# Two gathered blocks per expert in one tile, the shared expert ahead of routing, convolution biases added to x, fixed-point weights in the gated layer's columns

## The chip, the cores and the metric

The kernel runs on one core of a Trainium2 chip. The metric is the device time in microseconds (us) of one launch. The engines are named as in the profile: PE (TensorE; PEld are its weight loads), DVE (VectorE), ACT (ScalarE), POOL (GpSimd, which issues the indirect gathers) and SP (SyncE, which issues most other DMAs). An engine works through its instructions in a fixed order.

## The reference

A decoder of four layers on x of 8 batches x 256 tokens x 256 features. Each layer is attention, attention to a context, and a feed-forward part; after each the layer norm of x plus the result is taken:

```python
x = _layernorm(x + _L1_ffn_ref(x, gate_w, w_gate_up, w_down, shared_w_gate_up, shared_w_down))
...
x = _layernorm(x + _L2_ffn_ref(x, Wq, keys, down_embed, up_embed, Wg, Wu, Wd))
x = _layernorm(x + _L3_attn_ref(x, in_proj_w, in_proj_b, conv_w, ..., out_proj_w, out_proj_b, ln_w, ln_b))
x = _layernorm(x + _L3_xattn_ref(x, ctx_768, Wq, Wk, Wv, Wo, bo))
x = _layernorm(x + _L3_ffn_ref(x, w1, b1, w2, b2))
```

The parts that the change touches are these.

- `_L1_ffn_ref`: 32 experts with 4 chosen per token and room for 256 tokens each. An expert is silu(x Wg) * (x Wu), then Wd. A shared expert of the same form works on every token.
- `_L2_ffn_ref`: a gated feed-forward part (Wg, Wu, Wd with 1024 hidden columns), plus 4 heads x 8 single-row experts per token, taken from a table of 4096 rows.
- `_L3_attn_ref`: a projection to u and v, a short convolution and a linear recurrence over time, a projection out with a bias, then h = out + x, and (h - mean) * rsqrt(var + eps) * ln_w + ln_b. The outer line adds x once more and norms again.
- `_L3_ffn_ref`: 256 to 1024 to 256 with values rounded to multiples of 2^-8 and a piecewise linear gelu.

## The kernel before, in words

x stands in SBUF twice: `X` (tokens on partitions, 16 tiles of 128 x 256) and its transpose `xT`. `finish` (L183 and on) takes a sum z, norms it into `X`, turns it on PE and copies it to `xT` on ACT. The program is written in a framework that tracks the tiles and, at build, puts the instructions of each engine in order: by their place in the program, filling gaps with later ones that its own simulated timeline holds to be ready. So work of different layers stands interleaved on the engines, and the order doesn't change at run time. A pool's memory passes to a later pool when the tiles of the earlier one are released. Float32 matmuls show as two records each in the profile, transposes as one.

**Layer 1's feed-forward** (`l1_ffn`). `route1` makes one-hot matrices of the chosen experts on DVE, counts places with small matmuls (L1163, L1164), and finds with 16 x 4 matmuls (L1190, fed by `at` from DVE and ACT) which token goes to which place: `take` (L1197). Then the shared expert's hidden values `shT` are computed for eight chunks of 256 tokens: 8 matmuls of 128x128 by 128x256 to `ph` (L139, through `mm`; 64 records in all are `ph<-xT,sgu`), a silu on ACT (L1126) and a product on DVE (L1127). Then the loop over the 32 experts: SP loads the expert's weights `we` (L1266); `gathered_T` (L991 and on) is called twice, once per block of 128 tokens, and each call gathers 128 rows (L983, POOL), turns them with two transposes (L998) and copies them to `xeT` (L1000, ACT); 8 matmuls with 128 moving columns make `ph` (128x128 x512 records over all experts), silu and product make `hT`, two matmuls make `py`, DVE copies it to `y` (L1283), and SP stores it. After each fourth expert two tiles of the shared expert are projected down and added to `X` (L1291). The work pool has three buffers of each name, so three `xe` tiles are one and a half experts. DVE also works off the preparation of layer 2's quantized weights (L1877 to L1939) in the gaps.

**Layer 2's experts and layer 3's attention** (`l2_ffn`). For each of the 8 batches `expert_batches` runs the gated part (L1523 and on), then 64 gathers of table rows (L983, `rows`), dot products on DVE (L1511), `diag` on ACT (L1562) and matmuls into `po` (L1563). The convolution (`convolution_batches`) and the context attention (`context_batches`) of the batch before are Python generators, and a piece of them is issued between pieces of the experts (`next(later, None)`). In the convolution's last part the projection out has a bias matmul with one row (L141, through `mm`), then z = po + x (L1625), norm statistics, and five DVE instructions: two at L1628, and L1631, L1632 and L1633.

**Layer 3's feed-forward** (`fixed_point`). Its weights `w4` are loaded by SP after the loop over the batches, into the weight tile of which layer 2's weights are the last user (L125, L129). The pools `f3`, `f3w` and `f3p` come after those of the experts. Its matmuls are `ph<-xT,w`, its first activation is L1761, and it goes through 16 units, two for each batch.

Of the kernel before, what the change touches and what calls it, by code (L numbers as in the profile page):

```python
# [11 lines left out]
F32 = mybir.dt.float32  # L12
# [4 lines left out]
ALU = mybir.AluOpType  # L17
AX = mybir.AxisListType
PSUM = bass.MemoryType.PSUM
# [23 lines left out]
class Net:  # L43
# [947 lines left out]
    def gathered_T(self, xd, index, work):  # L991

        nc = self.nc
        xe = work.tile([P, D], F32, name="xe")
        self.gather_rows(xe, xd, index)
        pt = self.ps_t.tile([P, 2, P], F32, name="pt")
        for c in range(2):
            nc.tensor.transpose(pt[:, c, :], xe[:, c * P : (c + 1) * P], self.ident)  # L998
        xeT = work.tile([P, 2, P], F32, name="xeT")
        nc.scalar.copy(xeT, pt)  # L1000
        return xeT


# [226 lines left out]
    def l1_ffn(self, w):  # L1230
        nc, tc = self.nc, self.tc
        E, K, C = 32, 4, 256
        DROP = E * C
        with (
            tc.tile_pool(name="f1", bufs=1) as keep,
            tc.tile_pool(name="f1w", bufs=3) as work,
            ExitStack() as ctx,
        ):
            sgu = keep.tile([P, 2, 256], F32, name="sgu")
            nc.sync.dma_start(sgu, self.ins["l1f_sgu"].rearrange("p (c n) -> p c n", c=2))  # L1240
            sd = keep.tile([P, D], F32, name="sd")
            nc.sync.dma_start(sd, self.ins["l1f_sd"])
            xd, yd = self.xd1, self.yd1
            nc.gpsimd.partition_all_reduce(self.w_scale, self.w_sums[:, : len(L2X)], P, bass_isa.ReduceOp.add)
            with (
                tc.tile_pool(name="f1q", bufs=1) as pool,
                tc.tile_pool(name="f1r", bufs=1, space=PSUM) as ps,
            ):
                take = self.route1(E, K, C, pool, work, ps, keep)
            pool = ctx.enter_context(tc.tile_pool(name="f1l", bufs=1))  # L1250
            none = pool.tile([1, D], F32, name="none")
            nc.vector.memset(none, 0.0)
            nc.scalar.dma_start(yd[DROP : DROP + 1, :], none)
            with tc.tile_pool(name="f1p", bufs=2, space=PSUM) as ps:
                shT = pool.tile([P, NTOK], F32, name="shT")
                for o in range(0, NTOK, 256):
                    ph = ps.tile([P, 2, 256], F32, name="ph")
                    for m in range(2):
                        self.mm(
                            ph[:, m, :],  # L1260
                            [(sgu[:, c, m * P : (m + 1) * P], self.xT[:, c, o : o + 256]) for c in range(2)],
                        )
# [183 lines left out]
    def l2_ffn(self, w):  # L1446


        tc = self.tc
        with ExitStack() as ctx:  # L1450
            w3 = self.load(
                ("l3a_win", 2), ("l3a_wout", 2), ("l3x_wq", 2), ("l3x_wo", 4),
                rows=("l3a_bout", "l3a_ln_w", "l3a_ln_b", "l3x_bo"), spare=8 * D,
            )
            win, wout, wq, wo, bout, ln_w, ln_b, bo, fifth = w3
            pool3 = ctx.enter_context(tc.tile_pool(name="a3", bufs=1))
            ps3 = ctx.enter_context(tc.tile_pool(name="a3p", bufs=2, space=PSUM))
            convolve = self.convolution_batches((win, wout, bout, ln_w, ln_b), pool3, ps3)
            attend = self.context_batches((wq, wo, bo), pool3, ps3)
            later = iter(())  # L1460
            with (
                tc.tile_pool(name="f2", bufs=1) as pool,
                tc.tile_pool(name="f2w", bufs=2) as work,
                tc.tile_pool(name="f2p", bufs=2, space=PSUM) as ps,
            ):
                experts = self.expert_batches(w, fifth, pool, work, ps)
# [12 lines left out]
    def expert_batches(self, w, fifth, pool, work, ps):  # L1479
        nc = self.nc  # L1480
# [32 lines left out]
        def batch(b, later):  # L1513
# [9 lines left out]
            for f in range(FC):  # L1523
# [46 lines left out]

        return batch

    def convolution_batches(self, w, pool, ps):

        nc = self.nc
        win, wout, bout, ln_w, ln_b = w
# [1 line left out]
        decay = pool.tile([P, 2], F32, name="decay")  # L1578
        nc.scalar.activation(decay, self.col("l3a_logit_a"), AF.Sigmoid)
        affine = pool.tile([P, 2, D], F32, name="affine")  # L1580
        for n, row in enumerate((ln_w, ln_b)):
            pp = ps.tile([P, D], F32, name="s")
            nc.tensor.matmul(pp, lhsT=self.ones, rhs=row, start=True, stop=True)
            nc.scalar.copy(affine[:, n, :], pp)

        def batch(b):
            o = b * S
            oT = pool.tile([P, 2, S], F32, name="oT")
            for c in range(2):
                pp = ps.tile([P, 2, S], F32, name="s")  # L1590
# [26 lines left out]
            z = pool.tile([P, 2, D], F32, name="z3")  # L1617
            po = ps.tile([P, 2, D], F32, name="s")
            for j in range(2):
                self.mm(  # L1620
                    po[:, j, :], [(oT[:, c, j * P : (j + 1) * P], wout[:, c, :]) for c in range(2)], bias=bout
                )
            yield
            x = self.X[:, 2 * b : 2 * b + 2, :]
            nc.vector.tensor_tensor(z, po, x, ALU.add)  # L1625
            mv, r = self.norm_stats(z, 2)
            for j in range(2):
                nc.vector.tensor_scalar(  # L1628
                    z[:, j], z[:, j], mv[:, j, 0:1], r[:, j : j + 1], ALU.subtract, ALU.mult
                )  # L1630
            nc.vector.tensor_tensor(z, z, affine[:, 0:1, :].to_broadcast([P, 2, D]), ALU.mult)  # L1631
            nc.vector.tensor_tensor(z, z, affine[:, 1:2, :].to_broadcast([P, 2, D]), ALU.add)  # L1632
            nc.vector.tensor_tensor(z, z, x, ALU.add)  # L1633
            yield
            self.finish(2 * b, 1, z)
            yield
# [621 lines left out]
```

## Time and profile before

| what | value |
|---|---|
| median of three runs | 2654.91 us (2646.24 to 2655.16) |
| profiled execution | 2655.88 us, of which the span is 2654.1 us |
| mean granted TensorE clock | 0.885 |
| layer 1: end of context attention to `take` | about 919 to 958.5 us |
| layer 1: shared expert's records on PE | 958.5 to 975.9 us |
| layer 1: expert loop | 975.8 to 1111 us |
| layer 2's experts with layer 3's attention | about 1640 to 2410 us |
| the end: last batches' convolution and context, fixed point | 2395 to 2654 us |
| gathers of table rows | 412 + 100 of about 1.05 us, POOL |

The times in the second half are us from the start of the span. In a line of the timeline the columns are start, length, engine, line of the kernel, operation, out<-in, shapes and count; in brackets stands how long the engine sat idle before it and which engine's instruction ended that. A line of waits gives the total, the number of times and the longest. The chain that ended last is followed back from the last instruction, at each step to what released it.

### The profile page before, as it was taken

The numbers are of one execution on the slowest core, as the hardware profiler recorded it, in microseconds if no ns is written. First come the engines' busy times: TensorE is split into PE (matmuls) and PEld (weight loads), VectorE is DVE, ScalarE is ACT, GpSimd is POOL, SyncE is SP. The second block draws the span as 40 slices with busy tenths as digits, with TensorE's granted clock in tenths as the row PEclk, the third lists the DMA queues.
The fourth block names the chain that finished last, engine by engine and source line by source line (L and its number), as shares of the span: only waits on it lengthen the run. The fifth ranks groups of instructions, "written<-read, shape, count | busy, mean of one in ns | idle before, by whom it ended". The sixth has DMA issues, their size and how long they took to land.

```text
span 2654.1 us, 41230 instructions
## 1 busy us (share of the span) xinstructions
PE 2156.2 (81%) x14481; PEld 1564.3 (59%) x14481; DVE 1617.1 (61%) x5506; ACT 987.5 (37%) x2268; POOL 948.7 (36%) x988
## 2 busy tenths in 40 slices
PE   8988799699989879767787776678888788767796
PEld 5656688455566558634455355466666666545575
DVE  4665200466667686335676885477687687654676
ACT  2332233133333442213333353235445445332653
POOL 1021221311111124433310136576666765670122
PEclk9998799799999979968898777789889999877797
DMA  2001531200011137511101011111111122120000
GB/s 85 2 1 56 197 132 59 74 1 2 1 72 47 45 98 213 169 43 33 33 2 60 1 46 44 45 45 56 54 48 46 54 55 55 53 84 13 1 13 20
DMA packets 88639, 143.01 MB, mean 54 GB/s; under 512 B 33941, under 2 KB 55589, under 8 KB 86512
## 3 DMA queue, kind: packets, MB, share of 16 engines
q0 software_dynamic: 52288, 79.27, 10.2%
q1 hardware_dynamic: 33388, 57.37, 6.6%
q10 hardware_dynamic: 2756, 3.72, 0.4%
q8 instruction: 116, 1.90, 0.3%
q14 instruction: 91, 0.75, 0.1%
HBM read 246.87 MB, written 21.66 MB: 101 GB/s over the span
## 4 chain that ended last, share of the span: by engine, by line
PE 47%; DVE 25%; issue 9%; DMA 6%; POOL 5%; ACT 4%; another core or an unknown queue 4%; POOLq 0%; ACTq 0%; DVEq 0%
PE sc L139 6%; PE pp L139 6%; PE ph L139 5%; PE po L1563 5%; PE s L139 3%; PE sc L487 3%; PE py L139 3%; DVE low L520 2%; DMA xe<-xd,take 2%; PE pt L139 2%; DVE low L504 2%; DVE X L194 2%; DMA we<-in_l0f_experts_dram,wrow 2%; PE s L1702 1%
## 5 line engine op out<-in xcount | busy, mean ns | idle before, releaser
L983 POOL DMA_INDIRECT rows<-in_l2f_table_dram,index x412 | 431.3, 1047 | 241.2 <-issue 107.2
L139 PE MATMUL pp<-xT,w 128*128 128x256 f32 (+1 forms) x672 | 202.7, 441 | 34.3 <-issue 23.3
L1563 PE MATMUL po<-rows,diag 128*128 128x256 f32 x618 | 177.2, 422 | 43.8 <-ACT diag L1562 20.4
L139 PE MATMUL ph<-xeT,we 128*128 128x128 f32 x1248 | 183.4, 290 | 19.1 <-DMA we<-in_l0f_experts_dram,wrow 16.0
L595 POOL TENSOR_TENSOR aT<-sides,inv 128x256 f32<-128x256 f32 x64 | 46.7, 730 | 423.3 <-DVE sides L593 329.8
L139 PEld LDWEIGHTS ph<-xeT,we 128*128 128x128 f32 x1248 | 169.8, 201 | 38.7 <-DMA we<-in_l0f_experts_dram,wrow 17.3
L1511 DVE SCALAR_TENSOR_TENSOR junk<-rows,X 128x256 f32<-128x256 f32 x412 | 172.5, 419 | 15.6 <-remote 4.4
L139 PEld LDWEIGHTS pp<-xT,w 128*128 128x128 f32 x672 | 141.6, 219 | 66.7 <-issue 30.6
L1562 ACT ACTIVATE diag<-ident,dots 128x128 f32<-128x128 f32 x384 | 132.5, 395 | 114.2 <-PE po L1563 42.2
L180 PE MATMUL pt<-ident,X 128*128 128x128 f32 x352 | 74.8, 332 | 122.3 <-DVE X L194 105.2
L1563 PEld LDWEIGHTS po<-rows,diag 128*128 128x128 f32 x618 | 121.7, 207 | 79.4 <-issue 30.0
L983 POOL DMA_INDIRECT xe<-xd,take x87 | 84.8, 975 | 208.6 <-PE pt L998 83.0
L181 ACT COPY xT<-pt 128x512 f32<-128x512 f32 x88 | 51.4, 587 | 287.4 <-PE pt L180 228.7
L180 PEld LDWEIGHTS pt<-ident,X 128*128 128x128 f32 x352 | 47.9, 162 | 158.7 <-issue 71.3
L1104 DVE TENSOR_TENSOR y<-py,we 128x256 f32<-128x256 f32 x23 | 9.8, 425 | 200.4 <-PE py L139 200.4
L139 PE MATMUL py<-we,hT 128*128 128x256 f32 x496 | 129.9, 386 | 0.9 <-DVE hT L1127 0.9
L983 POOL DMA_INDIRECT w<-in_l2f_table_dram,index x100 | 104.6, 1046 | 51.7 <-issue 21.6
L559 ACT ACTIVATE e<-sc 128x512 f32<-128x512 f32 (+1 forms) x146 | 77.4, 602 | 99.6 <-PE sc L487 66.8
L1098 ACT ACTIVATE hT<-ph,we 128x128 f32<-128x128 f32 x184 | 65.8, 367 | 122.2 <-PE ph L139 92.6
L487 PE MATMUL sc<-kv,qv 32*128 32x128 f32 (+2 forms) x1520 | 103.5, 316 | 3.4 <-ACT e L559 1.9
L139 PE MATMUL sc<-xT,w 128*128 128x512 f32 x216 | 104.8, 635 | 1.4 <-ACT xT L181 1.4
L194 DVE TENSOR_SCALAR X<-z,ln_mv,rs_y 128x256 f32<-128x256 f32 x176 | 68.8, 434 | 59.5 <-POOL rs_y L150 57.9
(542 smaller groups left out, 5349.9 us busy)
## 6 DMA issues: line engine op xcount, KB each, us to landing
we<-in_l1f_experts_dram SPq DMA_DIRECT2D x32, 384.0 KB
yd<-y SPq DMA_DIRECT2D x32, 256.0 KB
rows<-in_l2f_table_dram,index POOLq DMA_INDIRECT x412
w<-in_l2x_w_dram SPq DMA_DIRECT2D x1, 4096.0 KB
v<-v SPq DMA_DIRECT2D x16, 243.8 KB
yd<-y SPq DMA_DIRECT2D x23, 128.0 KB
X<-in_x_dram SPq DMA_DIRECT2D x8, 256.0 KB
xd<-X ACTq DMA_DIRECT2D x8, 256.0 KB
```

Source lines behind the costliest of these rows:

```text
L139: self.nc.tensor.matmul(out, lhsT=lhsT, rhs=rhs, start=n == 0, stop=n == last and bias is None)
L180: nc.tensor.transpose(pt[:, c, j, :], self.X[:, i0 + j * step, c * P : (c + 1) * P], self.ident)
L194: nc.vector.tensor_scalar(self.X[:, i, :], z[:, j, :], mv[:, j, 0:1], r[:, j : j + 1], ALU.subtract, ALU.mult)
L487: nc.tensor.matmul(sc[: shape[0], part], lhsT=lhsT, rhs=rhs, start=mask is None, stop=True, skip_group_check=True)
L504: nc.vector.tensor_reduce(low5[:, r, :, :, 0], sc, AX.X, ALU.max, negate=True)
L520: nc.vector.tensor_reduce(low4[:, r, :, 0], sc, AX.X, ALU.max, negate=True)
L559: lambda r, sc: nc.scalar.activation(e0[m][:n0, r], sc, AF.Exp),
L983: self.nc.gpsimd.indirect_dma_start(out=out, out_offset=None, in_=table, in_offset=bass.IndirectOffsetOnAxis(ap=index, axis=0), **({} if r ...
L1098: nc.scalar.activation(hT[:, g + f, :], ph[:, f, :], AF.Gelu, bias=b1[:, g + f : g + f + 1])
L1511: nc.vector.scalar_tensor_tensor(junk, row, 1.0, self.X[:, i, :], ALU.mult, ALU.mult, accum_out=out)
L1562: nc.scalar.activation(diag, self.ident, AF.Copy, scale=dots[:, k : k + 1])
L1563: nc.tensor.matmul(po, lhsT=diag, rhs=rows[:, k, D:], start=False, stop=g + k == H * K - 2)
```

## The change

The change has four parts.

1. `l1_ffn`: the shared expert's hidden values are computed ahead of `route1`, from a PSUM pool of their own (two banks) that is open beside the pool of `route1`.
2. `gathered_T` takes all blocks of an expert at once: one `xe` tile with two gathers, four transposes into one PSUM tile, one copy; `ph` is made by 4 matmuls with 256 moving columns. Layer 0's experts call it with one block, as before.
3. `convolution_batches`: the projection's bias is spread over the partitions once at the beginning. At the start of each batch x + bias and x + ln_b are computed; at its end z = po + (x + bias), then (z - mean) * ln_w, then that * r + (x + ln_b), tile by tile.
4. `l2_ffn`: the fixed-point layer's weights are loaded into the columns of Wg, Wu and the keys, after the last batch's gated loop. Layer 3's weight tile has 13 x 256 spare columns in place of 8 x 256, for part 3.

```diff
     def gathered_T(self, xd, index, work):
...
-        xe = work.tile([P, D], F32, name="xe")
-        self.gather_rows(xe, xd, index)
-        pt = self.ps_t.tile([P, 2, P], F32, name="pt")
-        for c in range(2):
-            nc.tensor.transpose(pt[:, c, :], xe[:, c * P : (c + 1) * P], self.ident)
-        xeT = work.tile([P, 2, P], F32, name="xeT")
-        nc.scalar.copy(xeT, pt)
+        n = index.shape[1]
+        xe = work.tile([P, n, D], F32, name="xe")
+        for j in range(n):
+            self.gather_rows(xe[:, j, :], xd, index[:, j : j + 1])
+        pt = self.ps_t.tile([P, 2, n, P], F32, name="pt")
+        for j in range(n):
+            for c in range(2):
+                nc.tensor.transpose(pt[:, c, j, :], xe[:, j, c * P : (c + 1) * P], self.ident)
+        xeT = work.tile([P, 2, n * P], F32, name="xeT")
+        nc.scalar.copy(xeT, pt.rearrange("p c j n -> p c (j n)"))
...
     def l1_ffn(self, w):
...
+            shT = keep.tile([P, NTOK], F32, name="shT")
             with (
                 tc.tile_pool(name="f1q", bufs=1) as pool,
+                tc.tile_pool(name="f1s", bufs=2, space=PSUM) as ps2,
                 tc.tile_pool(name="f1r", bufs=1, space=PSUM) as ps,
             ):
+                for o in range(0, NTOK, 256):
+                    ph = ps2.tile([P, 2, 256], F32, name="ph")
+                    for m in range(2):
+                        self.mm(
+                            ph[:, m, :],
+                            [(sgu[:, c, m * P : (m + 1) * P], self.xT[:, c, o : o + 256]) for c in range(2)],
+                        )
+                    self.silu_mul(shT[:, o : o + 256], ph[:, 0, :], ph[:, 1, :], [P, 256], work)
                 take = self.route1(E, K, C, pool, work, ps, keep)
...
             with tc.tile_pool(name="f1p", bufs=2, space=PSUM) as ps:
-                shT = pool.tile([P, NTOK], F32, name="shT")
-                for o in range(0, NTOK, 256):
...
-                    self.silu_mul(shT[:, o : o + 256], ph[:, 0, :], ph[:, 1, :], [P, 256], work)
                 for e in range(E):
...
-                    xeT = [self.gathered_T(xd, take[:, 2 * e + n : 2 * e + n + 1], work) for n in range(2)]
+                    xeT = self.gathered_T(xd, take[:, 2 * e : 2 * e + 2], work)
                     ph = ps.tile([P, 2, 256], F32, name="ph")
                     for m in range(2):
-                        for n in range(2):
-                            self.mm(
-                                ph[:, m, n * P : (n + 1) * P],
-                                [(wgu[:, c, m * P : (m + 1) * P], xeT[n][:, c, :]) for c in range(2)],
-                            )
+                        self.mm(ph[:, m, :], [(wgu[:, c, m * P : (m + 1) * P], xeT[:, c, :]) for c in range(2)])
...
     def l2_ffn(self, w):
...
-                rows=("l3a_bout", "l3a_ln_w", "l3a_ln_b", "l3x_bo"), spare=8 * D,
+                rows=("l3a_bout", "l3a_ln_w", "l3a_ln_b", "l3x_bo"), spare=13 * D,
...
-            w4 = self.load(("l3f_w1", 2), ("l3f_w2", 8), rows=("l3f_b2",))
...
-            self.fixed_point(w4, pool, work, ps)
+            self.fixed_point(self.w4, pool, work, ps)
...
     def expert_batches(self, w, fifth, pool, work, ps):
...
                 if f % 2:
                     next(later, None)
+            if b == B - 1:
+                flat = [v.rearrange("p c n -> p (c n)") for v in (wg, wu)]
+                nc.sync.dma_start(flat[0], self.ins["l3f_w1"])
+                nc.sync.dma_start(flat[1], self.ins["l3f_w2"])
+                at, n = LAYOUT.rows["l3f_b2"]
+                row = keys.rearrange("p c n -> p (c n)")[0:1, :n]
+                nc.sync.dma_start(row, self.ins["rows"][:, at : at + n])
+                self.w4 = wg, flat[1].rearrange("p (f d) -> p f d", d=D), row
...
     def convolution_batches(self, w, room, pool, ps):
...
-        for n, row in enumerate((ln_w, ln_b)):
+        bias_all = room[:, :D]
+        for n, row in enumerate((ln_w, ln_b, bout)):
...
-            nc.scalar.copy(affine[:, n, :], pp)
+            nc.scalar.copy(affine[:, n, :] if n < 2 else bias_all, pp)
+        plus = room[:, D:].rearrange("p (a j d) -> p a j d", a=2, d=D)
...
         def batch(b):
             o = b * S
+            x = self.X[:, 2 * b : 2 * b + 2, :]
+            nc.vector.tensor_tensor(plus[:, 0], x, bias_all.unsqueeze(1).to_broadcast([P, 2, D]), ALU.add)
+            nc.vector.tensor_tensor(plus[:, 1], x, affine[:, 1:2, :].to_broadcast([P, 2, D]), ALU.add)
...
             for j in range(2):
-                self.mm(
-                    po[:, j, :], [(oT[:, c, j * P : (j + 1) * P], wout[:, c, :]) for c in range(2)], bias=bout
-                )
+                self.mm(po[:, j, :], [(oT[:, c, j * P : (j + 1) * P], wout[:, c, :]) for c in range(2)])
             yield
-            x = self.X[:, 2 * b : 2 * b + 2, :]
-            nc.vector.tensor_tensor(z, po, x, ALU.add)
+            nc.vector.tensor_tensor(z, po, plus[:, 0], ALU.add)
             mv, r = self.norm_stats(z, 2)
             for j in range(2):
-                nc.vector.tensor_scalar(
-                    z[:, j], z[:, j], mv[:, j, 0:1], r[:, j : j + 1], ALU.subtract, ALU.mult
+                nc.vector.scalar_tensor_tensor(
+                    z[:, j], z[:, j], mv[:, j, 0:1], affine[:, 0, :], ALU.subtract, ALU.mult
                 )
-            nc.vector.tensor_tensor(z, z, affine[:, 0:1, :].to_broadcast([P, 2, D]), ALU.mult)
-            nc.vector.tensor_tensor(z, z, affine[:, 1:2, :].to_broadcast([P, 2, D]), ALU.add)
-            nc.vector.tensor_tensor(z, z, x, ALU.add)
+                nc.vector.scalar_tensor_tensor(z[:, j], z[:, j], r[:, j : j + 1], plus[:, 1, j, :], ALU.mult, ALU.add)
             yield
```

More of the change, by code (lines that the diff above doesn't have):

```diff
@@ L1254, in l1_ffn @@
             with tc.tile_pool(name="f1p", bufs=2, space=PSUM) as ps:
-                shT = pool.tile([P, NTOK], F32, name="shT")
-                for o in range(0, NTOK, 256):
-                    ph = ps.tile([P, 2, 256], F32, name="ph")
-                    for m in range(2):
-                        self.mm(
-                            ph[:, m, :],
-                            [(sgu[:, c, m * P : (m + 1) * P], self.xT[:, c, o : o + 256]) for c in range(2)],
-                        )
-                    self.silu_mul(shT[:, o : o + 256], ph[:, 0, :], ph[:, 1, :], [P, 256], work)
                 for e in range(E):
@@ L1452, in l2_ffn @@
                 ("l3a_win", 2), ("l3a_wout", 2), ("l3x_wq", 2), ("l3x_wo", 4),
-                rows=("l3a_bout", "l3a_ln_w", "l3a_ln_b", "l3x_bo"), spare=8 * D,
+                rows=("l3a_bout", "l3a_ln_w", "l3a_ln_b", "l3x_bo"), spare=13 * D,
             )
-            win, wout, wq, wo, bout, ln_w, ln_b, bo, fifth = w3
+            win, wout, wq, wo, bout, ln_w, ln_b, bo, spare = w3
             pool3 = ctx.enter_context(tc.tile_pool(name="a3", bufs=1))
             ps3 = ctx.enter_context(tc.tile_pool(name="a3p", bufs=2, space=PSUM))
-            convolve = self.convolution_batches((win, wout, bout, ln_w, ln_b), pool3, ps3)
+            convolve = self.convolution_batches((win, wout, bout, ln_w, ln_b), spare[:, 8 * D :], pool3, ps3)
             attend = self.context_batches((wq, wo, bo), pool3, ps3)
@@ L1465, in l2_ffn @@
             ):
-                experts = self.expert_batches(w, fifth, pool, work, ps)
+                experts = self.expert_batches(w, spare[:, : 8 * D], pool, work, ps)
                 for b in range(B):
@@ L1571, in expert_batches, with convolution_batches @@
         return batch
-    def convolution_batches(self, w, pool, ps):
+    def convolution_batches(self, w, room, pool, ps):
         nc = self.nc
@@ L1619, in batch @@
             for j in range(2):
-                self.mm(
-                    po[:, j, :], [(oT[:, c, j * P : (j + 1) * P], wout[:, c, :]) for c in range(2)], bias=bout
-                )
+                self.mm(po[:, j, :], [(oT[:, c, j * P : (j + 1) * P], wout[:, c, :]) for c in range(2)])
             yield
-            x = self.X[:, 2 * b : 2 * b + 2, :]
-            nc.vector.tensor_tensor(z, po, x, ALU.add)
+            nc.vector.tensor_tensor(z, po, plus[:, 0], ALU.add)
             mv, r = self.norm_stats(z, 2)
             for j in range(2):
-                nc.vector.tensor_scalar(
-                    z[:, j], z[:, j], mv[:, j, 0:1], r[:, j : j + 1], ALU.subtract, ALU.mult
-                )
-            nc.vector.tensor_tensor(z, z, affine[:, 0:1, :].to_broadcast([P, 2, D]), ALU.mult)
-            nc.vector.tensor_tensor(z, z, affine[:, 1:2, :].to_broadcast([P, 2, D]), ALU.add)
-            nc.vector.tensor_tensor(z, z, x, ALU.add)
+                nc.vector.scalar_tensor_tensor(
+                    z[:, j], z[:, j], mv[:, j, 0:1], affine[:, 0, :], ALU.subtract, ALU.mult
+                )
+                nc.vector.scalar_tensor_tensor(z[:, j], z[:, j], r[:, j : j + 1], plus[:, 1, j, :], ALU.mult, ALU.add)
             yield
```

## The prediction

> **What bounds the kernel now.** I read the page's head first. No engine is full over the span, so the change has to be priced stage by stage.
>
> ```profile
> span 2654.1 us, 41230 instructions
> ...
> PE 2156.2 (81%) x14481; PEld 1564.3 (59%) x14481; DVE 1617.1 (61%) x5506; ACT 987.5 (37%) x2268; POOL 948.7 (36%) x988
> ...
> PE 47%; DVE 25%; issue 9%; DMA 6%; POOL 5%; ACT 4%; another core or an unknown queue 4%; POOLq 0%; ACTq 0%; DVEq 0%
> ```
>
> The reader sees PE on less than half of the chain that ended last. Three stages hold the edited lines. I cut them out with the view of busy time by windows.
>
> ```profile
> 929.00:942.00 13.00, 3.44 (x34) 2.16 (x34) 11.82 (x50) 4.39 (x19) 0.99 (x1) 0.50 0.47 162
> 942.00:958.00 16.00, 11.33 (x160) 8.08 (x158) 11.57 (x53) 14.21 (x34) 0.00 (x0) 0.50 0.00 1
> 958.00:976.00 18.00, 16.66 (x74) 14.22 (x75) 15.40 (x34) 5.12 (x13) 7.03 (x6) 0.90 0.15 45
> 976.00:1111.00 135.00, 120.36 (x842) 106.21 (x840) 74.25 (x140) 32.42 (x98) 55.89 (x58) 1.00 0.68 202
> 1640.00:2395.00 755.00, 596.09 (x2652) 464.49 (x2652) 521.54 (x2588) 319.88 (x852) 499.52 (x478) 0.88 0.20 54
> ```
>
> Columns: window, length, then PE, PEld, DVE, ACT and POOL busy us, granted clock, DMA share, GB/s. Routing (929 to 958) is DVE first (11.82 of 13), then ACT (14.21 of 16), with PE mostly idle at a granted clock of 0.50. From 958 PE is the engine with work. Next the timeline where routing hands over to the experts:
>
> ```profile
> 958.50 5.20 PE L139 MATMUL ph<-xT,sgu 128*128 128x256 f32 x16 [0.56 <-DVE take L1197]
> ...
> 963.54 0.66 PE L998 MATMUL pt<-ident,xe 128*128 128x128 f32 x4
> ...
> 965.39 10.53 PE L139 MATMUL ph<-xT,sgu 128*128 128x256 f32 x48
> ...
> 975.76 1.95 PE L139 MATMUL ph<-xeT,we 128*128 128x128 f32 x16
> ```
>
> Expert 0's rows are turned at 963.5 and copied by 964.7, but its matmuls start at 975.8: the shared expert's 64 records lie between. Then the waits inside the expert loop (975 to 1111; total us, times, longest):
>
> ```profile
> POOL xe L983 <- PE pt L998: 64.6, 32, 10.3
> ...
> PE pt L998 <- DMA xe<-xd,take: 12.1, 13, 1.8
> ...
> PEld ph L139 <- ACT xeT L1000: 6.0, 16, 0.6
> ```
>
> POOL waits for a free xe buffer (three of one block, so one and a half experts), and PE then waits 12.1 us for the gathers issued too late. Last, the end of the kernel, in the timeline:
>
> ```profile
> 2403.79 1.22 PE L141 MATMUL s<-w,ones 1*128 1x256 f32 x2
> ...
> 2411.03 0.74 DVE L1628 TENSOR_SCALAR z<-z,ln_mv,rs_y 128x256 f32<-128x256 f32 x2
> 2411.80 0.69 DVE L1631 TENSOR_TENSOR z<-z,affine 128x512 f32<-128x512 f32 x1
> 2412.53 0.69 DVE L1632 TENSOR_TENSOR z<-z,affine 128x512 f32<-128x512 f32 x1
> 2413.25 0.69 DVE L1633 TENSOR_TENSOR z<-z,X 128x512 f32<-128x512 f32 x1
> ...
> 2461.22 0.84 ACT L1761 ACTIVATE v<-ph,b 128x256 f32<-128x256 f32 x2 [0.86 <-DVE X L194]
> ```
>
> Here the convolution's bias matmul and five DVE passes stand on the only chain there is, and the fixed-point layer's first activation waits for an X (L194), not for its weights.
>
> **1. Shared expert ahead of routing.** Nothing is removed; 64 PE records, 8 silus and 8 products move. Removed from the path: expert 0 could start at 964.7 instead of 975.8, 11.1 us. Added to routing: 8 products of 0.42 us on a DVE that is full from 929 to 942 (3.4 us; some may run before 929, where DVE is busy 2.97 of 10), 8 silus of 0.39 us on ACT, idle 928.4 to 932.2, and table loads: the Exp of the gates (L1213, at 935.5) falls between silus, so two more of 1.28 us, on ACT while DVE is the bound. I take a slip of routing of 4 us. What warms PE also goes: the first 16 shared records took 5.20 us (0.325 each), the next 48 took 10.53 (0.219), so a cold start costs about 1.7 us, and after the change expert 0 pays it. Net 11.1 - 4 - 1.7, about **-5 us**. Bounds: -11.1 if routing hides it all; +4.6 if routing waits for the whole 15.7 us.
>
> By the Trainium skill, page "TensorE: Matmul & The Clock Gate", section "Part 1: The HAM clock gate", PE falls back to half clock after about 3.4 us of idleness, which speaks against this move; the two shared groups agree. By it the term stays at -5, without it -7.
>
> The Trainium skill, page "ScalarE: Activation LUTs", section "What ACT_TABLE_LOAD costs", counts a drain of about 1.38 us on top of each load of 1.28, 2.66 together. The trace disagrees: at 2475.81 a load begins 0.02 us after the previous ACT end and its silu begins 1.29 later. By the page two switches would be an estimated 5.3 us instead of 2.6.
>
> **2. Two blocks per expert in one tile.** Gathers stay 64 (0.95 us each and 0.30 between them on POOL: 80 us, below the loop's 135) and transposes stay 128. Gone: 32 ACT copies (2 x 0.37 becomes one 128x512 copy, 0.59 in the row of L181) and half of ph's records: 512 of 0.1115 us in the chain (x14 take 1.56) become 256 of 0.217 (py: x4 take 0.87), 57.1 against 55.6, so only 1.5 us. What counts is depth: three xe buffers now hold three experts. The 12.1 us of waiting for gathers go: a gather then has two to three experts' time, over 7 us, against the 4 to 5 us that one takes here. Of the 6.0 us on xeT I take half, since PE can turn the next expert early, but a matmul now waits for the whole 0.59 copy. Sum 12.1 + 1.5 + 3, about **-17 us**. Next in line is PE itself: ph 55.6, py 128 x 0.217 = 27.8, pt 128 x 0.11 = 14.1, the shared down-projection 32 x 0.217 = 6.9 and some 8 of other records: 112 us, a bound of -23. DMA has room: 202 GB/s becomes 231 over 118 us, and the busiest fortieth of this window moves 298. DVE's 74 us and the L2 weights' preparation, whose last step is at 1057.5, also fit. The other bound is rival C.
>
> **3. Convolution, eight batches.** Removed per batch: 4 bias records (0.87 us warm), and on DVE L1628, L1631 to L1633, 2.95 us in a row. Added: two 512-wide adds at the batch's beginning (0.69 each, as L1633) and four scalar_tensor_tensor of 256 (0.48 by L1558, 0.40 apart) where the 2.95 stood: 1.7. The adds run while PE and ACT turn X and DVE has nothing of this chain; uncovered they cost 1.4. So DVE carries +0.1 to +0.5 us per batch and the chain gets 1.2 shorter, 2 to 3 with the matmuls. While experts run (101.6 us per batch; 64 gathers at 1.30 are 83) the convolution is not what POOL waits for: I take -0.4 per batch, **-3 us** for seven; bounds -20 (all of it passes) and +12 (DVE is 69% busy in order, and POOL's stalls of 18 us per batch grow by a tenth).
>
> At the end it is exposed. Batch 6: L141 takes 0.63 (2401.23 to 2401.86) and 1.15 (2403.79 to 2404.94) at the low clock, 1.8 + 1.2 = 3.0, all on the path to 2461. Batch 7: 2 x 1.15 + 1.2 = 3.5, but the fixed-point layer runs beside it and I count half. **-5 us**; bounds 0 and -8.
>
> **4. Fixed-point weights.** Two loads and a row leave the queue of SP at 2364 (where SP had waited 19.4 us) and go behind the gated loop of batch 7, whose last product is at 2301.9. They wait there for PE's last reader of wg and wu; behind them on SP are only kT and v of batches 6 and 7 (2335.8 and later), used from 2424 on. The 2 MB collide with gathers either way, in a stage with a DMA share of 0.20. First use is the ph matmuls at 2410.8, which wait for PSUM of the last po, and v waits for X at 2461 as long as its pool lies over the experts' z. **0**; if a gather is late for the load, +3; the case in which it opens something is rival B.
>
> **Sum.** -5 - 17 - 3 - 5 = -30. The profiled execution took 2655.88 us (span 2654.1 and 1.8 around it), 1.0 above the median of 2654.91; less 30 and less that one, **2625**.
>
> **Rivals.** The order on each engine is fixed at build by a planner, so every edit can reorder what follows.
> - **A, given back:** the loop loses its 12 us, but routing slips by the move's whole gain, or POOL's stalls in the L2 experts grow by 2 us per batch. For it: DVE and ACT are full in routing, and stalls are spread over 40 waits. Against: 3.8 us of ACT idleness at 928 and the DVE room ahead of it. Part 1 is 0, the L2 batches +12: -17 - 5 + 12, **2645**.
> - **B, the end opens:** the experts' last z is ready at 2409.7 (L1566) but its X is written at 2460.5, behind the context layer's. If the new order writes it at once, the convolution of batch 7 and the fixed-point layer start up to 45 us earlier; half of that is filler work anyway. For it: DVE is busy 29 of 67 us there. Against: the same lag, 15 to 24 us, stands in every batch, so a cause in the program is likely. **2603**.
> - **C, slower: experts one after another.** Place: PE's order in the loop. Today the next expert's transposes stand before the present py. If with one tile per expert they come behind it, nothing covers the copy and silu: 0.45 (pt) + 0.8 (copy and its ends) + 1.74 (ph) + 2.06 (ph's end to py's end, as in the last expert, 1107.97 to 1110.03) = 5.05 us against 135/32 = 4.2: +27 over 32, less 5 for the move, at 2655 + 22 = **2677**. It decides once the serial sum exceeds 4.2 + 5/32. Against: three xe and two pt buffers allow the overlap.
> - **D, no effect of the tiles:** the gathers are late for another reason (DMA rate), so only parts 1 and 3 remain: **2642**.
>
> **Numbers.** Forecast (2612 to 2636) 0.60, A 0.15, B 0.10, C 0.07, D 0.08. The range leaves out C and part of A and B: 2600 to 2652. This kernel's measurement can tell about 0.5%, 13 us, from no change: the line is 2641.6. Faster: forecast, B and a third of A and D, 0.78. Same: the rest of A and D, 0.14. Slower: C and a little, 0.08.
>
> **What would show it.** Right: the first ph of an expert at about 970 with the sgu records before 945; PE waiting under 3 us for xe in the loop; POOL's longest wait for pt well under 10 us; the loop at 118 us; no L141 in the convolution; z to X one to two us shorter at the end. Wrong: take later than 965, ph waiting for xeT over 10 us, a period of the L2 batches off 101.6 by over 2 us, or v's first activation far from 2461 less 33.

## The result and the profile after

The changed kernel takes 2633.99 us (median of 20 runs, 2619.64 to 2649.25), the kernel before in the same series 2652.50 (median of 20, 2637.74 to 2663.78): a ratio of 0.9927, 95% interval 0.9910 to 0.9943, or 19.4 us less (15 to 24). The microseconds beside this and every ratio below are the ratio less one, times the median of the kernel before. The profiled execution after took 2646.68 us, which is 12.7 above its median, while that of before lay 3.4 above its own; so single stages of the two profiles are compared with care below. The page of the kernel after, span and the chain that ended last:

```profile
span 2644.9 us, 40493 instructions
...
PE 46%; DVE 25%; issue 10%; another core or an unknown queue 6%; ACT 5%; POOL 5%; DMA 4%; POOLq 0%; ACTq 0%; DVEq 0%
```

PE is still on less than half of the chain. The kernel after by windows (length, then PE, PEld, DVE, ACT, POOL busy, granted clock, DMA share, GB/s): shared expert, rest of routing, experts from the first to the last `y`, second layer's experts.

```profile
924.00:943.00 19.00, 17.00 (x96) 14.51 (x97) 13.24 (x52) 12.35 (x33) 0.00 (x0) 0.88 0.33 112
943.00:958.00 15.00, 10.23 (x162) 7.22 (x159) 11.02 (x49) 12.89 (x29) 0.00 (x0) 0.71 0.00 1
...
972.80:1083.00 110.20, 106.85 (x534) 88.81 (x534) 66.13 (x124) 27.60 (x60) 52.77 (x55) 1.00 0.82 245
...
1560.00:2403.00 843.00, 646.00 (x2807) 504.85 (x2808) 565.67 (x2832) 344.25 (x902) 534.01 (x512) 0.86 0.18 51
```

The reader sees the shared expert's records beside routing, an expert loop in which PE is busy for 106.85 of 110.2 us, and at the end of the list the surprise: the stage of the second layer's experts takes 843 us from its first gather to its last, where it took 815 before (1579.9 to 2394.9). The timeline of the kernel after at the hand-over, and its waits in the loop (total us, times, longest):

```profile
958.42 0.23 DVE L1200 SCALAR_TENSOR_TENSOR take<-found,base 128x64 uint32<-128x64 f32 x1 [1.36 <-ACT base L1198]
...
961.89 0.69 PE L1001 MATMUL pt<-ident,xe 128*128 128x128 f32 x2 [3.75 <-DMA xe<-xd,take]
...
965.79 3.62 PE L139 MATMUL ph<-xeT,we 128*128 128x256 f32 x8
```

```profile
POOL xe L983 <- PE pt L1001: 27.8, 11, 4.1
...
PE pt L1001 <- DMA xe<-xd,take: 6.1, 4, 3.8
```

The experts' matmuls start 7.4 us after `take` instead of 17.5, and POOL's wait for free buffers falls from 64.6 to 27.8 us, its longest from 10.3 to 4.1. The last `y` is at 1083.0 instead of 1110.1. The convolution of batch 6 in the timeline of the kernel after:

```profile
2390.59 0.69 DVE L1637 TENSOR_TENSOR z<-s,w 128x512 f32<-128x512 f32 x1 [1.27 <-PE s L139]
...
2392.70 0.45 DVE L1640 SCALAR_TENSOR_TENSOR z<-z,ln_mv,affine 128x256 f32<-128x256 f32 x1
...
2405.86 0.88 DVE L1643 SCALAR_TENSOR_TENSOR z<-z,rs_y,w 128x256 f32<-128x256 f32 x2
```

The bias matmul and three passes are gone. The norm as a whole isn't shorter here, though: it begins earlier, at 2390.6 instead of 2405.0, and its last part stands 13 us behind its first, among the dot products of the last gathers. So 27 us were won by the end of layer 1, and the end came 9.2 us earlier (2654.1 to 2644.9). Where did the rest go, and by which part?

### The profile page after: what moved, and what is told of

The parts are those of the page before. It is cut to its first block, busy times and chain, and to the rows that moved or that the text cites. A ratio compares the mean times of both kernels' runs of the same rounds, so it can differ in the third digit from the quotient of the medians.

```text
span 2644.9 us, 40493 instructions
## 1 busy us (share of the span) xinstructions
PE 2129.9 (81%) x14195; PEld 1549.3 (59%) x14195; DVE 1613.6 (61%) x5514; ACT 992.5 (38%) x2241; POOL 948.0 (36%) x988
## 4 chain that ended last, share of the span: by engine, by line
PE 46%; DVE 25%; issue 10%; another core or an unknown queue 6%; ACT 5%; POOL 5%; DMA 4%; POOLq 0%; ACTq 0%; DVEq 0%
PE sc L139 6%; PE ph L139 6%; PE po L1572 5%; PE pp L139 5%; PE py L139 3%; PE s L139 3%; PE sc L487 3%; DVE low L520 2%; DVE low L504 2%; PE pt L139 2%; DMA we<-in_l0f_experts_dram,wrow 2%; DVE X L194 2%; DVE junk L1511 2%; DVE ln_st L170 1%
## 5 line engine op out<-in xcount | busy, mean ns | idle before, releaser
L1572 PE MATMUL po<-rows,diag 128*128 128x256 f32 x618 | 188.6, 438 | 76.3 <-ACT diag L1571 41.4
L139 PE MATMUL ph<-xeT,we 128*128 128x128 f32 (+1 forms) x992 | 176.1, 320 | 18.7 <-DMA we<-in_l0f_experts_dram,wrow 14.7
L139 PEld LDWEIGHTS ph<-xeT,we 128*128 128x128 f32 x992 | 151.4, 201 | 40.2 <-DMA we<-in_l0f_experts_dram,wrow 16.1
L181 ACT COPY xT<-pt 128x512 f32<-128x512 f32 x88 | 51.5, 588 | 291.6 <-PE pt L180 232.0
L139 PE MATMUL py<-we,hT 128*128 128x256 f32 x496 | 129.5, 385 | 1.1 <-DVE hT L1130 1.1
L1107 DVE TENSOR_TENSOR y<-py,we 128x256 f32<-128x256 f32 x23 | 9.8, 425 | 196.0 <-PE py L139 196.0
```

Source lines behind the costliest of these rows:

```text
L139: self.nc.tensor.matmul(out, lhsT=lhsT, rhs=rhs, start=n == 0, stop=n == last and bias is None)
L1572: nc.tensor.matmul(po, lhsT=diag, rhs=rows[:, k, D:], start=False, stop=g + k == H * K - 2)
```

## The experiments

They ran on three chips, and one thing must be known to read them: the kernel before took 2520.0 us in the series of the first four (chip 1) and 2521.3 in that of the next four (chip 5), but 2669.1 in that of the last four (chip 3), near the 2652.5 of the result's series. Each ratio is within its own series. I call chips 1 and 5 group Q, and chip 3 together with the result's series group R.

**One or several parts.** Edits: the hunks of the named parts of the diff, the others left as before.

Parts 1 and 2:

> Parts 1 and 2 alone (layer 1's shared expert ahead of routing, two blocks per tile); convolution and fixed-point weights as before. Theory G (layer 1 is worth its whole -27 us, and the reordered convolution of part 3 gave some of it back in the second layer's expert batches): the last y of the loop 25 to 29 us earlier than before, batches at 101.6 +- 1.5 us as before, total about -24 us (2628). Rival N (the long batches of the profiled execution after the change were chance; the layer-1 parts are worth less than the profile shows because some of it is lost between the loop and layer 2's experts, and part 3 gains): last y as early, but a total of only -10 to -16 us.

Measured: 0.9922 (0.9898 to 0.9946), -19.7 us, between the two theories.

Parts 3 and 4:

> Parts 3 and 4 alone; layer 1 as before. Theory G: batches of layer 2's experts longer by 1 to 3 us each, the end 5 to 7 us shorter, total 0 to +10 us. Rival N: batches within 1 us of 101.6, total -3 to -8 us as the prediction's terms for parts 3 and 4 (-3 and -5) say. The last y stays at about 1110 us.

Measured: 0.9918 (0.9892 to 0.9943), -20.7 us. Both theories fall here: part 3 neither loses nor gains a little.

All but part 3:

> The changed kernel without part 3 (convolution as before). Theory G: faster than the changed kernel, about -24 us against before. Rival N: slower than the changed kernel, -12 to -15 us against before, with L141 in the convolution again and the end some 5 us longer.

Measured: 0.9933 (0.9909 to 0.9958), -16.9 us.

All but part 4:

> The changed kernel without part 4 (fixed-point weights loaded after the batches into the old weight tile). If part 4 costs nothing, as the prediction says: within 4 us of the changed kernel, -19 against before. If the 2 MB of loads beside the last batch's gathers cost or the early weights open something, 5 us or more off the changed kernel, and the difference lies after 2312 us in the trace.

Measured: 0.9836 (0.9809 to 0.9863), -41.3 us, twice the result. Either part 4 costs 20 us beside part 3, or the chips of group Q give more; the changed kernel on such a chip tells (below).

The kernel before:

> The kernel before, once more, for a profile. In the first four experiments, which share one series of runs, the kernel before took 2520 us where it took 2652 in the series of the result, with no edit between. Theory K (the two series ran on chips that differ in the second layer's expert stage alone): if this run belongs to the 2520 kind, the time up to layer 1's last y is within 5 us of the first profile's 1110, the batches take 87 us instead of 102, and POOL's stalls of 12 to 20 us per batch are gone. If it belongs to the 2652 kind, batches of 102 us again. Rival: all stages are shorter in proportion (1110 becomes 1055).

Measured: 2523.05 us, one run. Last `y` at 1111.2, as in the first profile (1110.1); batches of 86.4 to 88.5 us; POOL's stalls 2.4 us per batch at most. Theory K holds, but for one thing: the way from the last `y` to layer 2's first gather is shorter here too, by 12.6 us (457.2 against 469.8).

The changed kernel:

> The changed kernel, all four parts. Theory K with parts that add up (layer 1 -18 from the first experiment, convolution -22 from the fourth less the first, weights about +2): -36 to -40 us against a before of 2520 us, or -19 again against a before of 2652 us, where POOL waits for buffers and the convolution's gain is lost. Rival I (part 3 and part 4 disturb each other, whatever the chip): -17 to -22 us against a before of 2520, since part 4 added 22 us to the version without it.

Measured: 0.9847 (0.9828 to 0.9866), -38.6 us. The parts add up (-19.7, -21.2 and some 2), and rival I falls.

Part 3 alone:

> Part 3 alone. Against a before of 2520: -20 to -24 us, of which about 14 lie between the last expert's z and the fixed-point layer's first v, and the rest in the batches. Rival I: the same, since part 4 is not there. Against a before of 2652: the 14 us at the end, and batches that are longer by 1 to 3 us each: +0 to +10. The prediction's terms would have it at -8 on either.

Measured: 0.9916 (0.9899 to 0.9933), -21.2 us.

Part 1 alone:

> Part 1 alone: the shared expert's hidden values ahead of routing, one block per tile as before. The prediction's term: take 4 us later than before, first ph of an expert 7 to 11 us earlier, loop of 130 us as before, total -5 us. Rival (routing waits for nearly all of it): take 8 to 10 us later, the total within 3 us of zero, and the whole of the first experiment's -18 belongs to the tiles.

Measured: 0.9996 (0.9982 to 1.0009), -1 us: the rival. The timeline has `take` 7 to 9 us later and the first `y` at 981.3 against 981.7. (The loop behind it takes 134.8 us against 129.5 in this profile, of an execution 7.0 us above its median.) The profile of part 1 alone, by windows, and the waits of DVE in this window:

```profile
934.00:953.00 19.00, 16.97 (x96) 14.51 (x97) 13.39 (x52) 12.32 (x33) 0.00 (x0) 0.87 0.34 114
```

```profile
DVE shT L1127 <- ACT silu L1126: 3.4, 4, 1.6
DVE total L1215 <- ACT picks L1213: 1.2, 1, 1.2
```

For 19 us PE is nearly full with the shared expert (16.97) while routing's DVE is busy for 13.39: what ran in 13 us (11.82 busy) is drawn out. DVE itself isn't full now. In its fixed order the shared expert's products stand between routing's steps, and four of them wait there for a silu, 3.4 us in all; 1.2 more go on the Exp of the gates, which now stands behind a table load (before, from 929 to 942, one wait of 0.7).

**Depth alone.**

```diff
-        xe = work.tile([P, D], F32, name="xe")
+        xe = work.tile([P, D], F32, name="xe", bufs=6)
```

> The kernel before with six xe buffers of one block in place of three, and nothing else of the change: as many gathers in flight as part 2 allows, with the narrow records and two copies. Theory D (part 2 works through depth, as the prediction says: 12 of its 17 us): first to last y 130 us becomes 112 to 118, total -10 to -18 us. Rival R (wide records and one copy per expert do it): first to last y stays within 4 us of 130 and the total within 4 us of zero.

Measured: 0.9979 (0.9961 to 0.9996), -5.6 us; the loop from first to last `y` 119.3 us. It lies between the two theories. By windows over just that loop: the kernel before, this one, and the changed kernel without part 1 (below), one fence each.

```profile
980.00:1110.10 130.10, 115.56 (x810) 102.15 (x809) 69.52 (x131) 31.44 (x95) 54.95 (x57) 1.00 0.70 209
```

```profile
975.00:1094.30 119.30, 114.91 (x805) 102.09 (x808) 69.23 (x130) 30.06 (x95) 52.09 (x54) 1.00 0.73 225
```

```profile
982.00:1089.90 107.90, 105.87 (x533) 88.85 (x536) 59.16 (x111) 28.27 (x61) 51.82 (x54) 1.00 0.81 248
```

Depth takes PE's idle time from 14.5 to 4.4 us and leaves its work at 115; the tile takes 9 us of work out of the loop. Depth is worth 10.7 us of loop, the rest of part 2 another 11.4.

**Order at the norm.**

```diff
-            for _ in later:
-                pass
             self.finish(2 * b, 1, z)
+            for _ in later:
+                pass
```

> The changed kernel with the experts' norm of a batch issued before the rest of the layer-3 work of the batch before, instead of after it (two statements exchanged). Theory L (the chain of convolution, context and the experts' norm, one batch behind another, sets the time of this stage, 87 to 88 us per batch): the experts' X is written 2 to 10 us after z instead of 13 to 40, the link falls out of the chain, and the kernel is 10 to 30 us faster than the changed one (-48 to -68 against before where that one is at -38). Rival (the gathers on POOL set it, 86 us per batch, and what stands at the end is filler anyway): within 5 us of the changed kernel. It can also lose: the norm then stands ahead of the context's pieces on DVE, up to +10.

Measured: 0.9923 (0.9899 to 0.9947), -20.6 us, as the changed kernel. From z to X it is still 16 us in the mean (17.5 in the changed kernel), X still follows the context's X by 3 to 12 us: exchanging two statements did not move the instructions, which the program's planner orders: on DVE, ACT and POOL they stand in the very order of the changed kernel. So it tells nothing on the link itself, but it is a measurement of the changed kernel on chip 3.

**Chain cost.**

```diff
                 nc.vector.scalar_tensor_tensor(z[:, j], z[:, j], r[:, j : j + 1], plus[:, 1, j, :], ALU.mult, ALU.add)
+            for _ in range(4):
+                nc.vector.tensor_tensor(z, z, z, ALU.max)
```

> The changed kernel with four 512-wide passes over z that change nothing (maximum of z and z, some 0.7 us each) at the end of each batch's convolution: 2.9 us per batch put back on the layer-3 chain, 23 us in all, and the same on DVE. Theory L: nearly all of it passes, +18 to +25 us against the changed kernel. Rival (the prediction's: while experts run the convolution is not waited for, and only the last two batches count): +3 to +7 us.

Measured: 1.0007 (0.9987 to 1.0027), +1.9 us against before; 22 and 26 us above the two other changed kernels of its series (-20.6 and -23.8), 21 above the changed kernel's -19.4. Nearly all passes, as theory L has it. Two of the passes in the timeline of this kernel:

```profile
2193.81 0.68 DVE L1645 TENSOR_TENSOR z<-z 128x512 f32<-128x512 f32 x1
2194.75 0.69 DVE L1645 TENSOR_TENSOR z<-z 128x512 f32<-128x512 f32 x1
```

They stand 0.94 apart: between them DVE does a dot product of the experts. The price isn't that of the passes alone: the planner moved other instructions too. Of the 3148 instructions that DVE has in both kernels from layer 2's first gather on, at most 2405 stand in the same order.

**Without part 1.** Edit: the changed kernel with the shared expert after `route1`.

> The changed kernel without part 1: the shared expert's hidden values after routing, as before. By the run of part 1 alone (within 1 us of before): the same time as the changed kernel within 4 us. If the move is worth something once the tiles are deep (the gathers of the first experts land during the 16 us of shared work, so that the loop starts full): 4 to 8 us faster without part 1; by the prediction's term, 5 us slower.

Measured: 0.9911 (0.9892 to 0.9930), -23.8 us. The interval meets that of the changed kernel (0.9910 to 0.9943) and, in its own series, that of the tenth experiment (0.9899 to 0.9947); part 1 gains nothing here either. No version tried beats the changed kernel by more than the intervals.

**Where part 3's time lies.** From the traces I cut the stretch from the convolution's first `v` of batch 0 to that of batch 6 into three pieces, each summed over six batches: `v` to the convolution's X, on to the context's X, and on (over the experts' X) to the next `v`. Mean of the profiles, us:

| group, convolution | profiles | `v` to X | context | link | sum |
|---|---|---|---|---|---|
| Q, as before | 4 | 196.0 | 320.2 | 52.0 | 568.1 |
| Q, part 3 | 4 | 178.0 | 305.4 | 62.7 | 546.1 |
| R, as before | 2 | 261.0 | 334.0 | 73.8 | 668.8 |
| R, part 3 | 3 | 229.6 | 338.1 | 99.8 | 667.5 |
| R, part 3 and four passes | 1 | 254.6 | 333.4 | 94.3 | 682.2 |

The convolution itself gets shorter on both kinds of chip, by 18 and by 31 us, 3 to 5 per batch in the mean. In group Q the sum falls by 22 us. In group R the link grows by 26, and the gain is gone from the sum. The single sums in group R range over 14 to 20 us for like kernels, so no single pair there proves anything.

A cut at the last gather of table rows says where the gain comes out. Means of the same profiles, us:

| group, convolution | first gather to the end of the last | that to the end of the kernel | the last gather's end, counted from batch 6's first `v` |
|---|---|---|---|
| Q, as before | 699.7 | 253.6 | 17.2 |
| Q, part 3 | 694.8 | 234.4 | 37.0 |
| R, as before | 826.8 | 258.1 | 7.0 |
| R, part 3 | 841.6 | 240.9 | 24.9 |
| R, part 3 and four passes | 856.5 | 244.5 | 21.3 |

The kernel before and part 3 alone, on chip 5, by windows up to the end of the last gather and behind it:

```profile
1568.40:2267.70 699.30, 611.34 (x2837) 485.08 (x2838) 566.49 (x2828) 345.19 (x908) 534.80 (x512) 0.92 0.24 62
2267.70:2521.00 253.30, 199.10 (x822) 155.72 (x821) 154.11 (x329) 114.75 (x187) 50.64 (x35) 0.82 0.04 11
```

```profile
1569.30:2263.10 693.80, 600.97 (x2819) 482.42 (x2820) 569.18 (x2868) 346.07 (x910) 535.85 (x512) 0.93 0.24 62
2263.10:2498.60 235.50, 183.56 (x809) 148.57 (x807) 145.64 (x298) 114.41 (x187) 49.69 (x36) 0.86 0.04 12
```

Behind the last gather 17 to 19 us are won in both groups, and like kernels agree there within 2.3 us. The gathers themselves take 5 us less in group Q. In group R they take 15 us more, where like kernels differ by 18 to 22.

## Why the prediction was right, and where it was wrong

Sign and range held (2634 in 2600 to 2652; -19.4 against -30). That the total came out inside is partly luck. On the chips of the result parts 1 and 3 both gave less than forecast; in group Q part 1 gave next to nothing, part 3 gave 13 us more than forecast, and the total is -38.6.

- **Part 1, -5: wrong.** It is 0 (-1 alone; on chip 3 -23.8 without it and -20.6 with it, by the tenth experiment, with intervals that overlap). The step that failed is "I take a slip of routing of 4 us". Counted from layer 0's `take`, that of layer 1 came 7.5 us later (679.7 us, mean of eight profiles with the move, against 672.2, mean of six without), and 9.2 later in the run of part 1 alone. From `take` to the first `y` that run saved 9.2 (22.0 to 12.8), near the 9.4 of the forecast: nothing is left. The cold start came: in the profile after, expert 0's first eight records take 3.62 us and the next twelve 2.75, so 1.8 more. The rows had a part of the slip: DVE 11.82 of 13 and ACT 14.21 of 16 busy leave 3 us, and I hid more than that behind them. What no busy time shows is the waiting in a fixed order: DVE stands for 5.6 of the 19 us in the window above. Rival A's "routing slips by the move's whole gain" is what happened.
- **Part 2, -17: right.** By the first and eighth experiments -18.7; from first `ph` to last `y` 134 us became 117 in the profile after. Of its terms depth held in the loop (12.1 forecast, 10.7 measured); of the whole kernel it was 5.6, with an interval of 1 to 10. "1.5 records" and "3 xeT", 4.5 together, measured 11.4. In the loop the `ph` records went from about 57 to 55 us (512 at 0.112 from start to start, then 256 at 0.216). The x column shows more than halved `ph` records: between the kernel before and that without part 1, 31 others and 10 us of DVE work left the loop. These are pieces of layer 2's preparation, which the planner now has behind the loop. That part is moved, not saved: in group R the way from the last `y` to layer 2's first gather grew from 470 to 473 us (before, depth alone) to 477 to 481; in group Q from 457 to 458, to 459 to 460. That the moved pieces cause this growth is argued, not shown.
- **Part 3, -3 and -5: wrong in group Q, -21.2.** The step that failed is "while experts run the convolution is not what POOL waits for: I take -0.4 per batch". For the gathers that was near the truth: they gained 4.9 us in the whole stage, and at 1.05 us each and 0.30 between two, 64 of them are a floor of 86 us (the forecast counted 83). But it doesn't follow that the rest is hidden. The layer-3 chain trails the gathers and ends the kernel. The convolution got 18 us shorter in six batches, 3.0 in the mean as worked out for the exposed batch, the context's stretch 15 us shorter, the link 11 us longer. So the chain trails less: batch 6's convolution begins 37.0 instead of 17.2 us before the last gather ends, and 19 us come out behind that gather. The bound "-20 (all of it passes)" was the answer. POOL's waits on chip 5 say why the reading of POOL misled. The kernel before on chip 5, then the first profile, both over some seven batches:

```profile
POOL rows L983 <- PE po L1563: 12.8, 33, 2.0
```

```profile
POOL rows L983 <- PE po L1563: 53.4, 41, 5.0
```

  I took POOL's stalls for a sign that the convolution's time is hidden. But POOL stalls in the first profile and hardly on chip 5, and behind the gathers the same 17 to 19 us are won in both groups: how long POOL waits doesn't say what the chain is worth. The run of four passes, in group R, shows little hidden either: 2.9 us per batch cost 21, the moved instructions included. A rival stands untested here. With part 3 the planner puts DVE's other instructions in another order as well (of 3094 in both kernels from layer 2's first gather on, at most 2112 stand in the same order), so the -21.2 belongs to part 3 with its order; what the removed passes alone give isn't shown.
- **"-5 at the end": wrong in its place.** From batch 6's first `v` to the end it is 270.5 us before and 269.6 with part 3 alone (chip 5). The last z to the first `v` of the fixed-point layer did shrink, 51.5 to 38.4, but only because the convolution of batch 6 had begun 21 us earlier (2229.0 in place of 2250.5). From z to X, batch 6's norm even took longer with part 3 (23.6 us against 12.2), since it now runs beside the last gathers. A small slip in the forecast's own reading: the five passes are 2.91 us by its rows, not 2.95.
- **In group R part 3 was not run alone.** In the profile after, the first gather comes 19.9 us earlier (1560.0 against 1579.9), as much as the whole -19.4, so what is left for part 3 is small. Behind the last gather it wins 17 us there too; the gathers take it back. POOL's stalls grew from 125 to 154 us over the eight batches in the profile after: rival A's second mechanism, at 3.6 us per batch, with a longer execution than the median. Why the gathers lose in this group what the chain wins stays open. That four passes cost 21 us there while part 3 gained next to nothing is no contradiction if it is DVE's time that sets the gathers' pace there: part 3 leaves DVE's busy time as it was (1617.1 to 1613.6 us), the passes add to it (1633.0). This is argued, not shown.
- **Part 4, 0: right.** With against without it: +2.7 (sixth and fourth experiments), +2.8 (third and first), +0.5 (second and seventh), none beyond its interval, and inside the "+3".
- **Rivals.** C did not come: next transposes stand ahead of `py`, and PE is idle 2 to 4 us in the loop. D neither. B did not come and no run tried it: the last z of the experts still waits 38.3 us for its X, 50.7 before. Its argument had "the same lag, 15 to 24 us, stands in every batch"; in the profile before the lag is 12 to 24 us in the first six batches and 52 and 51 in the last two.
- **What I said would show it.** Right: first `ph` at 965.8 (about 970), the last sgu record at 942.9 (before 945), POOL's longest wait 4.1, the loop 117 (118), no L141. Wrong: waits for `xe` 6.1 (under 3; four waits, two of them the first expert's), a batch period of 105 in the profile after (101.6 within 2), the first `v` at 2454.5 against 2428, and z to X at the end longer instead of one to two us shorter (batch 6: 21.8 us in the profile after, 12.2 before).

## What to carry to other kernels

Where one engine sets the pace of a stage and a chain trails it, a saving on the chain needn't be hidden: it can come out whole behind the stage, if that chain ends the kernel. Price it at its full size and at nothing, keep both ends, and look at the time from the stage's last instruction to the end. Work moved ahead of a stage costs that stage its waits as well as its busy time: here 3.4 us of products on DVE, with their silus and table loads, came with a slip of routing of 7.5 to 9.2. What an edit of a loop takes out of the loop is to be looked for behind it too; here pieces of the next layer moved there.

## What the runs showed of the hardware

The same instructions in the same order took 2655.9 us in the first profile and 2523.1 on chip 5, and up to the end of layer 1 they are within 1.2 us (1110.1 and 1111.2). The difference lies behind: 13 us from there to layer 2's first gather, and 117 in the experts' stage. It isn't the price of the instructions: a dot product on DVE takes 0.42 us in the mean of every profile, a gather of table rows 1.01 to 1.08 in the mean of every batch of all. Some 60 of the 117 us are time in which PE, DVE and ACT all stand: stretches over 1.5 us of that kind sum up to 76 us in the expert stage of the first profile and 16 in that of chip 5. They are 90 in the profile after, 50 to 83 in those of chip 3, and 4 to 16 in group Q. Where the rest of the 117 us goes wasn't taken apart. One of these stretches, in the first profile and at the same place on chip 5:

```profile
1597.36 1.22 PE L1544 MATMUL po<-w,hT 128*128 128x256 f32 x2
...
1604.14 0.38 ACT L1126 ACTIVATE silu<-pp 128x256 f32<-128x256 f32 x1 [8.51 <-remote]
```

```profile
1582.97 0.36 ACT L1126 ACTIVATE silu<-pp 128x256 f32<-128x256 f32 x1
...
1585.29 0.70 PE L1544 MATMUL po<-w,hT 128*128 128x256 f32 x2
```

On chip 5 the silu starts before that matmul. In the first profile it starts 5.6 us after the matmul's end (1598.58), with nothing recorded between on PE, DVE or ACT, only gathers on POOL. Most such stretches end with an instruction that waits for a PE result. What holds it back isn't in the traces, and no run took it apart. Missing PE records aren't it: the first profile has 14481, as many as weight loads and ten more than that of chip 5. One more difference stands in the profiles: all eight of group Q tell for a part of the table gathers when their rows landed (2.7 to 2.9 us after the issue, median), and the six of group R for none, so late landings aren't ruled out.
